# Layer 0's value product and its fillers in four TensorE tiles of 128 by 32 instead of two of 128 by 64

## The chip, the cores and the metric

The kernel runs on one NeuronCore of a Trainium2 chip. The metric is device time in microseconds. In three runs the kernel before took 2806.13 to 2808.9 us, with a median of 2807.47 us.

The engines are named as the profile names them: PE is TensorE's matmul, PEld its weight load, DVE is VectorE, ACT is ScalarE, POOL is GpSimd, and SP the queue that issues nearly all transfers. A name such as L514 is line 514 of the kernel.

TensorE's array has 128 rows (the contraction) and 128 columns (the partitions of the output). It can be used whole, or split into tiles: the profile's "128\*64" is a tile of 128 rows and 64 columns, two of which lie side by side, "128\*32" is one of four, "64\*64" one of four in a square, "32\*64" one of eight. Each instruction of the program addresses one tile, and tiles of one shape can run at once.

## What is computed

Two layers of cross-attention on a batch of four, all in float32. `x` is (4, 1024, 512), the context is (4, 1024, 384). Both layers have 16 heads; layer 0's are 64 wide, layer 1's 32 wide.

```python
def layer0(x, context):
    h = layernorm(x) * gamma + beta
    Q = (h @ Wq).reshape(B, NQ, 16, 64)
    K = (context @ Wk).reshape(B, NC, 16, 64)
    V = (context @ Wv).reshape(B, NC, 16, 64)
    attn = softmax(einsum('bihd,bjhd->bhij', Q, K)) * 64 ** -0.5
    vals = einsum('bhij,bjhd->bihd', attn, V).reshape(B, NQ, 1024)
    return x + vals @ Wo + bo

def layer1(x, context):
    xn = x * rsqrt(mean(x * x) + 1e-5) * norm_w
    q, k, v = xn @ wq, *split(context @ wkv)          # 16 heads of 32
    q, k = l2norm(rotate(q)), l2norm(rotate(k))
    attn = softmax(q @ k.T * sqrt(32))
    return x + (attn @ v) @ wout

out = layer1(layer0(x, context), context)
```

## The kernel before, in words

The four samples are worked through one after the other, each with layer 0 and then layer 1. In the profile a sample takes some 695 us: layer 0 about 450, layer 1 about 245.

**Layer 0** goes over 8 pairs of heads (a pair fills 128 partitions) and, within a pair, over 8 blocks of 128 queries. One step of `Attention0` (lines 462 to 491) makes the scores of one block for both heads (line 453, in 64\*64 tiles, 512 columns at a time), DVE takes each row's maximum (478), ACT the exponential (479), POOL divides by the sum (484), DVE turns 32 by 32 squares over (487), and 16 transfers regroup the squares of two blocks into the transposed probabilities `eT` (498). `product` (506 to 522) multiplies two blocks' `eT` with the values: for each of 8 blocks of 128 keys and each of the two heads, the head's 64 columns of `v` are the stationary operand, and 256 queries stream through (line 514). The two heads fill the two column halves of the array. The moving operand `eT[:, j, :, :, k * 32 : (k + 1) * 32]` is read in runs of 32 numbers. Products follow the scores by some blocks and are called in odd steps (490).

**Fillers.** After its scores, each step lets PE do other work while DVE and ACT work on the softmax. In the first layer's pairs that go by rows (`by_rows`, line 899), even steps do row-split products (`rows`, line 186, in 64\*64 tiles like the scores), and odd steps the values of a pair ahead. In the other pairs `work.fill` takes units from a queue, each with a price in microseconds written by hand (0.86 for a 512-column step, 0.66 for a block of values, 0.44 for half a step). The prices are constants and decide which units are taken in which step.

**The helper.** All these fillers but the row-split ones and the transposes go through `matmul` (167 to 172). It cuts the output's 128 columns into `which["cols"]` tiles and issues one product for each. `which["cols"]` is 2 while layer 0 is built and is set to 4 at line 1054 for layer 1, whose own product (line 741) has 32 columns for each of four heads, and back to 2 at line 1125. The helper serves the projections of queries and keys (`pqT`, `pkT`), the values (`pv`), the output product (`po`), and layer 1's projections (`k_p`, `q_p`); some of layer 1's first ones (`k_p`, and `pv` from `wkv`) are built while layer 0 still runs.

**Layer 1** goes over 4 groups of four heads, 256 queries and 256 keys at a time: scores in 32\*64 tiles (692), exponential on ACT (702), sums of probabilities on DVE (711 to 715), product with the values in 128\*32 tiles (741), with the second half of layer 1's projections, the output product and the next sample's first work as fillers (`self.u.fill`, 706).

All instructions of one engine run in the order of the program. One written float32 product becomes two weight loads and two MATMUL instructions in the profile.

Of the kernel before, what the change touches and what calls it, by code (L numbers as in the profile page):

```python
# [38 lines left out]
P = 128  # L39
# [7 lines left out]
HD0 = 64  # L47
# [61 lines left out]
def xattn_kernel(ctx: ExitStack, tc: tile.TileContext, a: dict, out: bass.AP):  # L109
# [13 lines left out]
        return ps_s.tile(list(shape), F32, tag="s", name=name)  # L123


    which = {"n": 0, "from": 0, "cols": 2, "reads": 0}
    read = [0, 0, 0, 0]
    held = {}

    def bank(name):  # L130

        which["n"] = min(range(which["from"], 4), key=lambda n: read[n])
        res = ps_f.tile([P, 512], F32, tag=f"f{which['n']}", name=name)
        held[id(res)] = res, which["n"]
        read[which["n"]] = float("inf")
        return res

    def free(pp, late=0.5):

        which["reads"] += 1  # L140
        read[held.pop(id(pp))[1]] = work.clock + late + 1e-6 * which["reads"]

    def evac(dst, src):
        nc.scalar.copy(dst, src)
# [8 lines left out]
    cols = const.tile([P, 3, NQ], F32, name="cols")  # L153
# [282 lines left out]
    BQ = 2  # L436
    r = [slice(j * HD0, (j + 1) * HD0) for j in range(2)]

    class Attention0:
# [66 lines left out]
        def product(self):  # L506
            p, q, pr, eT = self.blocks.popleft()
            W = BQ * P
            if q == 0:
                pr["vals"] = sb.tile([P, S], F32, tag="vals", bufs=4, name=f"vals0_{self.b}_{p}")  # L510
            av = bank(f"av_{self.b}_{p}_{q}")
            for k in range(NT):
                for j in range(2):
                    nc.tensor.matmul(  # L514
                        av[r[j], :W].rearrange("p (t a i) -> p t a i", t=BQ, a=4),
                        pr["v"][:, k, r[j]],
                        eT[:, j, :, :, k * 32 : (k + 1) * 32],
                        start=k == 0,
                        stop=k == NT - 1,
                    )  # L520
            evac(pr["vals"][:, q * W : (q + 1) * W], av[:, :W])
            free(av)
# [371 lines left out]
    for b in range(B):  # L894
# [14 lines left out]
        for p in range(NPAIR):  # L909
            later = 17.3 * (p == 0)  # L910
            other = []
            if p in by_rows:
                if p < 2:
                    outs = tail
                elif p % 2 == 0:
                    i = p // 2 - 1
# [3 lines left out]
                        lambda n, i=i: wo[i][:, n % 2, :],  # L920
# [45 lines left out]
            elif p % 2 == 0:  # L966
                i = p // 2 - 1
# [3 lines left out]
                    lambda n, i=i: wo[i][:, n % 2, :],  # L971
# [3 lines left out]
            if p == 6:  # L975
                kq, v = {}, []
# [7 lines left out]
                k = rotated_chains(lambda kq=kq: kq["k"], ct, NC_, lambda k, wk=wk: wk[:, k, :], f"k1_{b}_0", RowScratch())  # L984
# [15 lines left out]
            n = 7 * (p == 0)  # L1000
# [6 lines left out]
            for i in range(NT):  # L1007
# [10 lines left out]
                n = NT * (2 - p if p < 2 else NPAIR - p) - i  # L1018
# [32 lines left out]
        work.add(flat(outs[4:7]) + q[0][2] + outs[7])  # L1051
        work.drain()

        which["from"], which["cols"] = 1, 4
        att1 = Attention1(b, work)
        o = [
            sb.tile([P, S], F32, tag="vals", bufs=4, name=f"o1_{b}_{g}") if g < 2 else None
# [8 lines left out]
        for half in range(2):  # L1066
            n = 0
# [49 lines left out]
            kT, qT, v = kT1, qT1, att1.v1  # L1117
# [4 lines left out]
        att1.ended = True  # L1122
        att1.add_up()
        att1.quotient()
        which["from"], which["cols"] = 0, 2
        if b == B - 1:
            tail = flat(adds[1][4:])
        else:
# [42 lines left out]
```

## Time and profile before

| | |
|---|---|
| median of three runs | 2807.47 us |
| the profiled execution | 2810.92 us, of which the span from first to last instruction is 2808.9 us |
| granted TensorE clock | 0.999 of full speed |
| line 514 (product with the values) | 4096 MATMULs of 128\*64, mean 382 ns |
| its weight loads | 4096 of 64 columns, mean 137 ns |
| line 453 (layer 0's scores) | 4096 MATMULs of 64\*64, mean 598 ns |
| line 172 (the helper) in 128\*64 | 5008 MATMULs, of 128, 256 and 512 columns |
| line 172 in 128\*32 (layer 1) | 4800 MATMULs, of 128, 256 and 512 columns |
| line 741 (layer 1's product) | 4096 MATMULs of 128\*32, mean 386 ns |
| its weight loads | 4096 of 32 columns, mean 109 ns |
| transfers | 349.90 MB, mean 125 GB/s |

The instructions overlap: a MATMUL lasts 380 ns from its start to its modelled end, while the next on the same tile starts earlier. The mean of one is thus not what one costs, and the busy time of a group is the union of its instructions.

### The profile page before, as it was taken

To read this page: it belongs to the slowest core of one execution; us is meant where nothing else is said; L and a number is where in the kernel's file an instruction comes from. 1 tells how busy PE (TensorE), PEld (TensorE's weight loads), DVE (VectorE), ACT (ScalarE), POOL (GpSimd) and SP (SyncE) were. 2 spreads that over 40 slices of the span, in tenths; PEclk is the share of its full clock that TensorE was granted. 3 is DMA by queue.
4 is the path that set the end of the run, shared out by engine and by line. 5 is a ranking of instruction groups with operands and counts; after the bars stand their busy time and mean duration, and the time that the engine had idled before them with its cause. 6 is when DMAs were issued, how large, how long until landed. Compare 5 with 4: busy or idle time off the path is not lost.

```text
span 2808.9 us, 82714 instructions
## 1 busy us (share of the span) xinstructions
PE 2781.3 (99%) x35344; PEld 1391.0 (50%) x35344; DVE 2242.8 (80%) x3010; ACT 1436.3 (51%) x2323; POOL 945.1 (34%) x776
## 2 busy tenths in 40 slices
PE   9999999999999999999999999999999999999999
PEld 4444445555444444554454444455445444445543
DVE  5677786899777778699877777869987777886988
ACT  4444443766544444476644444446664444445665
POOL 2343354430234335342023433444202343353410
PEclk9999999999999999999999999999999999999999
DMA  5788777010388877501048888750105887874000
GB/s 141 175 196 188 183 168 162 23 38 27 73 204 193 191 186 167 143 23 38 27 95 203 196 188 190 157 128 23 38 27 119 200 196 180 188 162 110 3 3 32
DMA packets 177615, 349.90 MB, mean 125 GB/s; under 512 B 37600, under 2 KB 93152, under 8 KB 177248
## 3 DMA queue, kind: packets, MB, share of 16 engines
q1 hardware_dynamic: 176848, 344.42, 51.9%
q8 instruction: 278, 4.55, 0.7%
q14 instruction: 89, 0.73, 0.1%
q10 hardware_dynamic: 400, 0.20, 0.0%
HBM read 67.64 MB, written 8.39 MB: 27 GB/s over the span
## 4 chain that ended last, share of the span: by engine, by line
PE 74%; DVE 7%; ACT 2%; issue 1%; DMA 1%; POOL 0%; SPq 0%; DVEq 0%; ACTq 0%
PE s L453 13%; PE av L514 12%; PE s L692 8%; PE pv L172 7%; PE av L741 6%; PE po L172 6%; PE po L194 4%; PE pqT L194 4%; PE pkT L194 3%; PE k_p L172 3%; PE q_p L172 2%; DVE both L711 2%; ACT e L702 1%; PE pqT L172 1%; PE pkT L172 1%
## 5 line engine op out<-in xcount | busy, mean ns | idle before, releaser
L478 DVE TENSOR_REDUCE m<-s 128x1 f32<-128x1024 f32 x512 | 602.8, 1219 | 359.3 <-PE s L453 356.2
L702 ACT ACTIVATE e<-s 128x1024 f32<-128x1024 f32 x512 | 496.7, 1022 | 289.1 <-PE s L692 246.1
L479 ACT ACTIVATE e<-s,m 128x1024 f32<-128x1024 f32 x256 | 282.8, 1109 | 465.5 <-DVE m L478 281.3
L453 PE MATMUL s<-qk 64*64 64x512 f32 x4096 | 516.8, 598 | 3.2 <-ACT raw L479 0.9
L484 POOL TENSOR_SCALAR raw<-raw,li 128x1024 f32<-128x1024 f32 x256 | 286.1, 1118 | 693.5 <-DVE li L483 685.0
L479 ACT ACTIVATE raw<-s,m 128x1024 f32<-128x1024 f32 x256 | 285.1, 1114 | 369.2 <-DVE m L478 366.0
L514 PE MATMUL av<-eT,v 128*64 128x256 f32 x4096 | 470.1, 382 | 1.8 <-DMA eT<-e 1.7
L484 POOL TENSOR_SCALAR e<-e,li 128x1024 f32<-128x1024 f32 x256 | 286.3, 1120 | 472.1 <-DVE li L483 269.4
L514 PEld LDWEIGHTS av<-eT,v 128*64 128x64 f32 x4096 | 285.0, 137 | 228.2 <-issue 64.2
L711 DVE TENSOR_TENSOR both<-e 128x512 f32<-128x512 f32 x512 | 338.0, 692 | 55.6 <-ACT e L702 53.6
L487 DVE STREAM_TRANSPOSE e<-e 128x1024 f32<-128x1024 f32 x256 | 309.9, 1228 | 0.2
L487 DVE STREAM_TRANSPOSE e<-raw 128x1024 f32<-128x1024 f32 x256 | 309.9, 1228 | 0.0
L692 PE MATMUL s<-q,k 32*64 32x256 f32 x8192 | 302.6, 388 | 7.2 <-ACT e L702 5.9
L453 PEld LDWEIGHTS s<-qk 64*64 64x64 f32 x4096 | 150.8, 132 | 255.9 <-issue 197.7
L692 PEld LDWEIGHTS s<-q,k 32*64 32x64 f32 x8192 | 157.3, 131 | 163.7 <-ACT e L702 80.2
L172 PE MATMUL pv<-wv,cT 128*64 128x128 f32 (+1 forms) x3360 | 189.6, 273 | 1.5 <-ACT k L590 1.4
L172 PEld LDWEIGHTS pv<-wv,cT 128*64 128x64 f32 (+1 forms) x3360 | 174.0, 132 | 31.3 <-issue 15.0
L713 DVE TENSOR_TENSOR both<-both 128x1024 f32<-128x1024 f32 x128 | 162.6, 1271 | 4.4
L194 PE MATMUL pqT<-hT,w 64*64 64x512 f32 x1408 | 159.5, 589 | 0.0
L741 PE MATMUL av<-e,rest 128*32 128x256 f32 x2048 | 137.8, 387 | 0.0
L741 PE MATMUL av<-e,v 128*32 128x256 f32 x2048 | 137.0, 385 | 0.0
L172 PE MATMUL q_p<-wq,hT 128*32 128x256 f32 (+1 forms) x1920 | 126.1, 379 | 0.0
(99 smaller groups left out, 3071.8 us busy)
## 6 DMA issues: line engine op xcount, KB each, us to landing
eT<-e SPq DMA_DIRECT2D x2048, 128.0 KB, 2.4
xr<-in_x_dram SPq DMA_DIRECT2D x32, 256.0 KB, 4.1
w<-in_Wq_dram SPq DMA_DIRECT2D x32, 256.0 KB, 3.3
x<-in_x_dram SPq DMA_DIRECT2D x32, 256.0 KB, 3.0
wo<-in_Wo_dram SPq DMA_DIRECT2D x16, 512.0 KB, 4.3
out_dram<-x SPq DMA_DIRECT2D x32, 256.0 KB, 2.5
c<-in_ctx_dram SPq DMA_DIRECT2D x32, 192.0 KB, 3.7
wv<-in_Wv_dram SPq DMA_DIRECT2D x32, 192.0 KB, 3.4
```

Source lines behind the costliest of these rows:

```text
L172: nc.tensor.matmul(o[rr], lhsT[:, rr], rhs, start=start, stop=stop)
L194: nc.tensor.matmul(o["pp"][cc], o["lhsT"](k)[rr, cc], o["rhs"](k)[rr], start=first and k == 0, stop=not first and k == n - 1,)
L453: nc.tensor.matmul(sc[j][part : part + HD0, kb * 512 : (kb + 1) * 512], pr["qT"][r[j], i * P + part : i * P + part + HD0], pr["kT"][r[j], ...
L478: nc.vector.tensor_reduce(m[:, j : j + 1], sc[j], AX.X, ALU.max, negate=True)
L479: nc.scalar.activation(e[j], sc[j].rearrange("p (g s) -> p g s", g=4), AF.Exp, bias=m[:, j : j + 1], accum_out=l[:, j : j + 1])
L484: nc.gpsimd.tensor_scalar(e[j], e[j], li[:, j : j + 1], HD0**-0.5, ALU.mult, ALU.mult)
L487: self.turn = [lambda j=j: nc.vector.transpose(self.e[:, :, i % BQ * 2 + j, :], e[j]) for j in range(2)]
L514: nc.tensor.matmul(av[r[j], :W].rearrange("p (t a i) -> p t a i", t=BQ, a=4), pr["v"][:, k, r[j]], eT[:, j, :, :, k * 32 : (k + 1) * 32], ...
L692: nc.tensor.matmul(sc[j // 2][part : part + HD0, j % 2, c, :], kT[rr, g, k * P + part : k * P + part + HD0], qT[rr, g, qb * WQ : (qb + 1) ...
L702: nc.scalar.activation(e, sc[u], AF.Exp, scale=float(np.sqrt(np.float32(HD1))))
L711: nc.vector.tensor_add(into[:, 2 * u : 2 * u + 2, :], es[u][:, :, 0, :], es[u][:, :, 1, :])
L741: nc.tensor.matmul(self.av[rr, 0, :], v[g][:, 2 * kk + c, rr], es[j // 2][:, j % 2, c, :], start=first and c == 0, stop=end and c == 1,)
```

## The change

The column width of the helper `matmul` is 4 throughout, where it was 2 in layer 0 and 4 in layer 1. The product of layer 0 is written with four 32-column pieces for each block of keys instead of two 64-column ones; the pieces 0 and 1 take the first head's probabilities, 2 and 3 the second's.

```diff
-    which = {"n": 0, "from": 0, "cols": 2, "reads": 0}
+    which = {"n": 0, "from": 0, "cols": 4, "reads": 0}
...
             for k in range(NT):
-                for j in range(2):
+                for f in range(0, P, 32):
                     nc.tensor.matmul(
-                        av[r[j], :W].rearrange("p (t a i) -> p t a i", t=BQ, a=4),
-                        pr["v"][:, k, r[j]],
-                        eT[:, j, :, :, k * 32 : (k + 1) * 32],
+                        av[f : f + 32, :W].rearrange("p (t a i) -> p t a i", t=BQ, a=4),
+                        pr["v"][:, k, f : f + 32],
+                        eT[:, f // HD0, :, :, k * 32 : (k + 1) * 32],
                         start=k == 0,
                         stop=k == NT - 1,
                     )
...
-        which["from"], which["cols"] = 1, 4
+        which["from"] = 1
...
-        which["from"], which["cols"] = 0, 2
+        which["from"] = 0
```

## The prediction

> **What bounds the kernel now.** I read the page's first and fourth parts, to see which engine sets the end.
>
> ```profile
> span 2808.9 us, 82714 instructions
> PE 2781.3 (99%) x35344; PEld 1391.0 (50%) x35344; DVE 2242.8 (80%) x3010; ACT 1436.3 (51%) x2323; POOL 945.1 (34%) x776
> ...
> PE 74%; DVE 7%; ACT 2%; issue 1%; DMA 1%; POOL 0%; SPq 0%; DVEq 0%; ACTq 0%
> PE s L453 13%; PE av L514 12%; PE s L692 8%; PE pv L172 7%; PE av L741 6%; PE po L172 6%; PE po L194 4%; PE pqT L194 4%; PE pkT L194 3%; PE k_p L172 3%; PE q_p L172 2%; DVE both L711 2%; ACT e L702 1%; PE pqT L172 1%; PE pkT L172 1%
> ```
>
> TensorE (PE) is busy almost without a gap, and the chain of waits runs through it. A busy PE may be one that runs slowly, so I then asked for the busy time by stage: one sample's layer 0 (735 to 1175 us) and the layer 1 behind it.
>
> ```profile
> core 0: us, PE busy (x) PEld busy (x) DVE busy (x) ACT busy (x) POOL busy (x), PEclk, DMA share, GB/s
> 735.00:1175.00 440.00, 439.53 (x4212) 220.22 (x4214) 341.96 (x457) 193.80 (x366) 179.89 (x158) 1.00 0.78 182
> 1182.00:1426.00 244.00, 241.97 (x4611) 122.71 (x4600) 213.87 (x288) 162.75 (x210) 52.45 (x33) 1.00 0.10 29
> ```
>
> In layer 0, where nearly all of the change lies, PE is busy for 439.53 of 440 us at full clock, and the next engine (DVE) for 342. So what a visit of PE to the changed column tiles costs is what counts. That needs both kinds of tile, which the groups by shape set side by side (busy us, then mean ns of one):
>
> ```profile
> L514 PE MATMUL av<-eT,v 128*64 128x256 f32 x4096 | 470.1, 382 | 1.8 <-DMA eT<-e 1.7
> L172 PE MATMUL pv<-wv,cT 128*64 128x128 f32 x2784 | 171.2, 273 | 1.4 <-ACT k L590 1.4
> L741 PE MATMUL av<-e,v 128*32 128x256 f32 x2048 | 137.0, 385 | 0.0
> L172 PE MATMUL pv<-wv,cT 128*32 128x128 f32 x576 | 18.4, 273 | 0.1
> ```
>
> One written product stands as two MATMULs: line 514 makes 4 x 8 x 4 x 8 x 2 = 2048 and shows 4096. The busy times here are unions of overlapping instructions, and short bursts inflate them, so they can't be divided by counts; starts can. From the single starts in the trace, the same column tile takes its next instruction every 216 ns at 256 columns, 109 ns at 128 and 429 ns at 512, **in 128*64 and in 128*32 alike** (call that a slot). Timeline rows, start and length, show the same with the ends of each visit:
>
> ```profile
> 383.45 1.95 PE L453 MATMUL s<-qk 64*64 64x512 f32 x16
> 385.32 3.67 PE L514 MATMUL av<-eT,v 128*64 128x256 f32 x32
> 388.83 0.83 PE L172 MATMUL pv<-wv,cT 128*64 128x128 f32 x12
> 389.58 1.95 PE L453 MATMUL s<-qk 64*64 64x512 f32 x16
> ...
> 517.02 1.07 PE L741 MATMUL av<-e,v 128*32 128x256 f32 x16
> 518.02 1.09 PE L283 MATMUL pth<-ident,xn 128*128 128x128 f32 x8
> ...
> 653.25 1.49 PE L172 MATMUL pv<-wv,cT 128*32 128x128 f32 x48
> 654.68 1.12 PE L692 MATMUL s<-q,k 32*64 32x256 f32 x32
> ```
>
> A 128*64 visit: 385.32 to 389.58 is 4.26 us, and 16 slots of 0.216 and 6 of 0.109 make 4.11, so 0.15 is left over. A 128*32 visit: 517.02 to 518.02 is 1.00, four slots make 0.86, and 0.14 is left over. The 48 values in 128*32 take 1.43 for 12 slots (1.31) and the way out. Nothing grows with length; only the ends of a visit differ.
>
> **The change part by part.** *What it converts.* L514's 4096 MATMULs, and all 128*64 rows of the helper at L172: 2784 + 512 + 576 + 768 + 128 + 96 + 128 + 16 = 5008 (pv of both layers' weights, po of vals, k_p, pqT, pkT, q_p, po of o). That makes 9104 more MATMULs and as many weight loads, 18,208 instructions. "All fillers" is not literally so: the row-split products of L194 (64*64) and the transposes (128*128) are not built by this helper and stay. No DMA, no evacuation and no wait is added or moved, and the planner's prices are constants, so the order of work stays.
>
> *Inside a visit: 0.* Half the columns per tile, twice the tiles, the same slot: 216, 109 and 429 ns in both.
>
> *Entering.* The first weight load of a new shape can't hide, and the first MATMULs are longer by it:
>
> ```profile
> L514 PE MATMUL av<-eT,v x4096: 378/379/431, 62.6 to 2562.6; 128*64 128x256 f32 x196
> L741 PE MATMUL av<-e,v x2048: 379/379/404, 491.1 to 2690.5; 128*32 128x256 f32 x187
> ```
>
> 431 - 379 = 52 against 404 - 379 = 25 ns; in starts, the first slot is 51 longer in 128*64 and 24 in 128*32. Entering gains 27 ns.
>
> *Leaving.* From the last MATMUL's start, the next shape starts one slot plus 88 to 95 ns later, whichever two shapes meet (93 from L514 to 64*64, 93 from L741 to 128*128, 93 in the three passages from 128*32 to 64*64). But the tiles of one slot start 6.7 ns apart, so the last of four starts 20 ns after the first, and of two 6.7: leaving loses 13.5 ns. Net per visit 27 - 13.5 = 13.5 ns gained, as 151 against 137 ns left over.
>
> The Trainium skill, "TensorE: Matmul & The Clock Gate", section "Measured speedup vs the span model", puts the spacing of tiles at about 4 ns; by it, as an estimate, leaving would lose 8 and the net be 19 ns, but the starts above measure 6.7. The same page speaks against the change in "Wait — 56ns, not 53.3ns?": with hardware decode off the sequencer spends about 62 ns per MATMUL. An estimate by it: four MATMULs would take 248 ns, 32 more in each of 2400 slots of 256 columns and 139 more in each of 1776 of 128, some 324 us slower; the values in 128*32 refute it here with 109 ns per four.
>
> *How many visits.* Merging PE's MATMULs in order of time by tile shape gives 203 visits in 128*64: 170 entered from 64*64, 32 from a transpose, one from 128*32. 203 x 13.5 = 2.74 us. Where PE waits for something else before its next such visit, the gain is swallowed: 43 of them have a wait over 30 ns there, and 160 x 13.5 = 2.16. I take **2.5 us**. The wait that swallows is line 453's for its score bank (ACT behind DVE); that is what is late next.
>
> *Not shown before, with bounds.* (a) The entry from 64*64 into 128*32 does not occur before. All entries into 128*32 are 22 to 25 and all exits of 64*64 86 to 88, so +-7 ns on 170 visits, +-1.2 us; I take 0. (b) Line 514 reads its moving operand in runs of 32 numbers, and four tiles will read it where two did. Nearest rows: L514 with two tiles 216, L741 with four tiles on unbroken rows 216. Between nothing and a slot doubled (2048 x 0.216 = 442 us); I take nothing, as both nearest rows give 216. (c) Instruction supply: the slower rival below, 0 to 24 us; I take 0. (d) Downwards: if entering cost nothing at all, 203 x 51 ns = 10.4 us less.
>
> Sum, against the profiled execution: span 2808.9, with 2.0 around it 2810.92, becomes 2806.4 and 2808.4. That execution stands 3.45 us above the median 2807.47 of the runs (2806.13 to 2808.9), so I take the difference from the median: **2805.0 us**, 0.09% down.
>
> **The rivals.** *Slower: instruction supply.* The page has
>
> ```profile
> q8 instruction: 278, 4.55, 0.7%
> ```
>
> 278 packets of 16 KB for 70,688 PE instructions are one per 256, and 18,208 more need 71 more. Beside it stand DMA engines 78% busy in layer 0 against 10% in layer 1. In one place of one sample's layer 1 (1352 us) the values in 128*32 stop for 450 instead of 109 ns, with no releaser, right after a fetch that started late; the other samples don't stop there. If every added fetch cost these 0.34 us, 71 x 0.34 = 24 us: **2829**. It makes the kernel slower by 0.2% from 24 of the 71 on (8.1 us over 0.34). Against it: layer 0 now has 8426 PE instructions in 440 us and would have some 12,980, 256 in 8.7 us; layer 1 draws 9211 in 244 us, 256 in 6.8 us, and runs through. A fetch takes 0.9 to 1.8 us in the trace even under layer 0's traffic.
>
> *Slower: the strided operand* of (b): from 4 ns per slot (8.2 us over 2048) it would decide; at 10 ns **2825**.
>
> *No gain at all.* PE's head start is lost each time at line 453's score bank: **2807.5**. For it: those 43 visits. Against it: all of PE's waits in layer 0, by the starts, come to some 33 of 1800 us.
>
> *More gain*: with nothing of the entry left, **2797**. Against it: the 24 ns that L741 still pays.
>
> **How the numbers follow.** The forecast has 0.72, no gain 0.08, supply 0.10, the strided operand 0.04, more gain 0.06. A measurement of this kernel can tell about 0.2%, 5.6 us, from no change. The forecast's own range is 2802 to 2808 (2.2 to 2.7 gained, +-1.2 of (a), and the spread of the runs). The whole range, 2800 to 2811, takes in a third of the larger gain below and some ten late fetches above. Faster by over 0.2%: 0.07; within: 0.79 (forecast and no gain, less a point of tail); slower: 0.14.
>
> **What would show it.** L514 as 128*32 x8192 with a longest first MATMUL near 404 in place of 431; weight loads near 110 ns, not 137; slots still 216 and 109; visits with 0.137 left over; PE x44448; some 349 fetches in the page's third part. Supply would show as stops inside visits with no releaser, the strided operand as L514 slots over 216 with L172's at 216. I am wrong if the slot itself moves, for then thousands of slots count where I counted 203 ends.

## The result

The changed kernel takes 2818.49 us (median of five runs, 2814.63 to 2819.58), against 2807.36 us (2806.13 to 2808.9) before. The ratio is 1.0035 with a 95% interval of 1.0022 to 1.0049: 11 us slower, where 2.5 us faster was forecast, and above the range.

The page of the changed kernel, its first, third and fourth parts (shares of the span by engine, the queue of PE's instruction fetches, the chain of waits):

```profile
span 2816.5 us, 100922 instructions
PE 2776.8 (99%) x44448; PEld 1352.9 (48%) x44448; DVE 2243.4 (80%) x3010; ACT 1436.2 (51%) x2323; POOL 944.8 (34%) x776
...
q8 instruction: 349, 5.72, 0.9%
...
PE 67%; DVE 8%; SPq 4%; DMA 3%; ACT 2%; issue 2%; POOL 0%; DVEq 0%; ACTq 0%
PE s L453 11%; PE av L514 11%; PE s L692 8%; PE av L741 6%; PE pv L172 6%; PE po L172 6%; SPq L498 4%; PE pqT L194 3%; PE po L194 3%; PE pkT L194 2%; PE q_p L172 2%; DMA eT<-e 2%; PE k_p L172 2%; DVE both L711 2%; ACT e L702 1%
```

PE has the 44448 MATMULs and the queue the 349 fetches that were forecast, and PE's busy time fell by 4.5 us (2781.3 before) while the span grew by 7.6. The chain shows what is new: SP's issue of the regrouping transfers (SPq L498) and their flight (DMA eT<-e), 6% of the span between them, neither of which stood among the chain's lines before. Two groups of the changed kernel (busy us, mean ns of one, idle before):

```profile
L514 PE MATMUL av<-eT,v 128*32 128x256 f32 x8192 | 468.6, 380 | 14.3 <-DMA eT<-e 9.4
L172 PE MATMUL pv<-wv,cT 128*32 128x128 f32 x6144 | 190.4, 273 | 1.4 <-ACT k L590 1.4
```

The product's busy time fell by 1.5 us, but PE stood idle before it for 14.3 us in place of 1.8, most of it until a transfer into `eT` landed. The view of line 514 (duration min/median/max) has the shorter entry that was forecast:

```profile
L514 PE MATMUL av<-eT,v x8192: 376/379/404, 61.4 to 2570.2; 128*32 128x256 f32 x200
```

404 where it was 431. So PE does what was reckoned, and something before it got later. The view of line 498, the regrouping's issues and waits on SP, first before the change, then after it:

```profile
L498 SPq DMA_DIRECT2D eT<-e x2048: 507/590/2217, 45.4 to 2551.7; - x187
L498 SPq EVENT_SEMAPHORE  x128: 17/1304/21187, 16.1 to 2542.2; - x128
...
  POOL e L484: 189.5, 47
  ACT e L479: 121.3, 31
  PE av L514: 1.7, 2
...
DMA to landing us min/median/max: 2.2/2.4/7.0
```

```profile
L498 SPq DMA_DIRECT2D eT<-e x2048: 507/590/2290, 44.2 to 2562.7; - x187
L498 SPq EVENT_SEMAPHORE  x128: 17/966/21174, 15.8 to 2552.1; - x128
...
  POOL e L484: 231.0, 58
  ACT e L479: 137.0, 36
  PE av L514: 9.4, 10
...
DMA to landing us min/median/max: 2.2/2.9/7.3
```

SP issues 16 transfers of 0.59 us for every two blocks and then waits for the next ones to be written. The median of that wait fell from 1304 to 966 ns. A transfer takes 2.9 us to land in the median, not 2.4. POOL, ACT and PE stand with longer waits for it (us, times). For POOL and ACT this only changes which wait ended last: all waits before these two groups come to 463.4 and 465.5 us before the change and to 461.4 and 463.8 after it. What grew is PE's. SP's issuing is no busy time in the profile's first part, so the engine table of the prediction did not have this queue in it. From the single starts in the two traces, within the 22 pairs by rows:

| | before | after |
|---|---|---|
| time of a pair | 52.6 us | 52.8 us |
| SP issuing, per pair | 42.0 us | 43.5 us |
| PE fetches, per pair | 4.14 | 5.86 |
| issues of eT longer than 0.8 us, whole kernel | 119 | 171 |
| from eT's last landing to its product, median | 1.81 us | 1.32 us |
| products that start late, of 128, and their delay in all | 5, 2.1 us | 22, 15.8 us |

A product counts as late where it starts over 15 ns behind the 90 ns that PE takes from the scores to the next shape where nothing interferes. Each late one starts within 0.5 us of the last landing in its `eT`, so that this is what it waited for. 1.5 us more of issue for 1.72 more fetches is 0.87 us for each. Of the 171 long issues, 165 have a fetch of PE's instructions that began during them or up to 1.5 us before; of the 1877 short ones 140. Before the change it is 112 of 119 and 81 of 1929.

PE's own account, made by taking the slots, entries and exits of the prediction off the starts of all visits: entries cost 36.9 us instead of 42.3 and exits 113.7 instead of 111.1, together 2.8 us less, and what remains, the waits, 77.1 instead of 67.5, 9.6 more. That is the result's sign and nearly its size: 6.8 of the 7.6 us of these two executions. The late products alone make 13.7 us more; PE's other waits fell by some 4. Line 453 does not wait longer than before: the idle time before it was 3.2 us and is 3.0.

### The profile page after: what moved, and what is told of

Read it like the earlier page. It is cut to its first block, busy times and chain, and to the rows that moved or that the text cites. A ratio compares the mean times of both kernels' runs of the same rounds, so it can differ in the third digit from the quotient of the medians.

```text
span 2816.5 us, 100922 instructions
## 1 busy us (share of the span) xinstructions
PE 2776.8 (99%) x44448; PEld 1352.9 (48%) x44448; DVE 2243.4 (80%) x3010; ACT 1436.2 (51%) x2323; POOL 944.8 (34%) x776
## 4 chain that ended last, share of the span: by engine, by line
PE 67%; DVE 8%; SPq 4%; DMA 3%; ACT 2%; issue 2%; POOL 0%; DVEq 0%; ACTq 0%
PE s L453 11%; PE av L514 11%; PE s L692 8%; PE av L741 6%; PE pv L172 6%; PE po L172 6%; SPq L498 4%; PE pqT L194 3%; PE po L194 3%; PE pkT L194 2%; PE q_p L172 2%; DMA eT<-e 2%; PE k_p L172 2%; DVE both L711 2%; ACT e L702 1%
## 5 line engine op out<-in xcount | busy, mean ns | idle before, releaser
L479 ACT ACTIVATE e<-s,m 128x1024 f32<-128x1024 f32 x256 | 283.0, 1110 | 463.8 <-DVE m L478 259.4
L514 PE MATMUL av<-eT,v 128*32 128x256 f32 x8192 | 468.6, 380 | 14.3 <-DMA eT<-e 9.4
L514 PEld LDWEIGHTS av<-eT,v 128*32 128x32 f32 x8192 | 262.8, 110 | 259.4 <-issue 72.5
L172 PE MATMUL pv<-wv,cT 128*32 128x128 f32 x6144 | 190.4, 273 | 1.4 <-ACT k L590 1.4
L172 PEld LDWEIGHTS pv<-wv,cT 128*32 128x32 f32 x6144 | 171.3, 110 | 32.9 <-issue 14.7
L172 PE MATMUL q_p<-wq,hT 128*32 128x256 f32 x2048 | 126.1, 379 | 0.0
```

The lines of the kernel that those rows point to most:

```text
L172: nc.tensor.matmul(o[rr], lhsT[:, rr], rhs, start=start, stop=stop)
L479: nc.scalar.activation(e[j], sc[j].rearrange("p (g s) -> p g s", g=4), AF.Exp, bias=m[:, j : j + 1], accum_out=l[:, j : j + 1])
L514: nc.tensor.matmul(av[f : f + 32, :W].rearrange("p (t a i) -> p t a i", t=BQ, a=4), pr["v"][:, k, f : f + 32], eT[:, f // HD0, :, :, k * 3 ...
```

## The experiments

**Theory A**: the 71 added fetches hold up SP's issues, `eT` lands later, and PE, ACT and POOL wait for it. **Theory B**: four tiles that read the moving operand slow the transfers. The prediction's own rival was a third: PE starves of instructions.

### More instructions without another tile: split256 and after_split256

```diff
-            for kb in range(2):
+            for kb in range(4):
...
-                            sc[j][part : part + HD0, kb * 512 : (kb + 1) * 512],
+                            sc[j][part : part + HD0, kb * 256 : (kb + 1) * 256],
...
+                for h in range(2):
+                    hh = slice(h * 256, (h + 1) * 256)
...
-                        o["rhs"](k)[rr],
-                        start=first and k == 0,
+                            o["rhs"](k)[rr, hh],
+                            start=first and k == 0 and h == 0,
```

> The kernel before, its two-tile columns kept, but the scores (L453) and the row-split fillers (L194) are written in halves of 256 columns: 15,936 more PE instructions, some 62 more fetches of 256 instructions, no tile shape changed. PE's own price: a slot of 512 columns takes 429.3 ns and two of 256 take 431.5, on some 2000 slots, +4.3 us. Theory A (each fetch holds up SP's issue of the regrouping transfers, eT lands later, L514 waits): +4.3 and about 62 x 0.18 us (12.6 us over the 71 fetches of the change), 2823 us (2816 to 2832), with issues of eT longer than 0.8 us up from 119 to some 165. Theory B (four tiles reading the moving operand slow the transfers): only PE's price, 2812, long issues as before.

> The changed kernel with the same halves of 256 columns: another 62 fetches on top of the 71. Theory A: SP has no room left in layer 0's pairs by rows, so each fetch costs between 0.18 and 0.8 us: 2818.5 + 4.3 + 11 to 50, 2834 to 2870. Theory B: 2823, PE's price alone.

split256 took 2828.94 us, a ratio of 1.0069 (1.0057 to 1.0082), within theory A's range; but its time alone does not tell the theories apart. Its starts show a price on PE that was not reckoned: some 84 places in the row products with 60 ns more and some 72 passages from the scores with 50 ns more. With the slots that is about 13 us, the greater part of the loss. The rest goes the way of theory A: 14 products start late, by 7.9 us in all, where it was 5 and 2.1, and the long issues rise to 145, for 340 fetches, though no tile is changed. after_split256 took 2847.53 us, 1.0130 (1.0114 to 1.0145), within theory A's range too. That is 18.6 us over split256, where the change alone costs 11: the same 71 fetches seem to cost more where `eT` already lands later. 41 products start late, by 28.1 us in all, and from eT's landing to the product it is 0.69 us in the median.

### Where the loss is: outside4 and inside4

```diff
-            later = 17.3 * (p == 0)
-            other = []
+            later, other, which["cols"] = 17.3 * (p == 0), [], 2 if p in by_rows else 4
...
-                for j in range(2):
+                for f in range(0, P, P // which["cols"]):
+                    ff = slice(f, f + P // which["cols"])
```

inside4 has 4 and 2 in place of 2 and 4. Behind the pairs of layer 0, outside4 goes on with 4, and inside4 with 2 until layer 1 begins.

> Four tiles only outside layer 0's pairs by rows (the other pairs, layer 1's first work and the tail), two within them: some 8,400 of the 18,208 added instructions (33 fetches) and some 115 of the 203 visits. Theory A (fetches hold up SP, where SP has no room): SP waits 5 to 20 us per pair there, so the fetches cost nothing and PE's 115 x 13.5 ns = 1.5 us show: 2804 to 2810. Theory B (four tiles slow the transfers everywhere): half of the loss, 2812 to 2815.

> Four tiles only within layer 0's pairs by rows, two elsewhere: some 9,900 added instructions (38 fetches), some 88 visits (-1.2 us). Theory A: the whole loss, as SP waits only 3 to 4 us of a pair's 53 here: 2816 to 2823. Theory B: the other half, 2812 to 2815.

outside4: 1.0001 (0.9992 to 1.0010), no difference, as theory A has it and theory B hasn't. inside4: 1.0015 (1.0006 to 1.0023), 4 us slower: the sign and the place are theory A's, the size is half of its lower bound. The two don't add up to the change's 11 us.

### SP relieved: before8 and after8

```diff
-            for g in range(4):
-                for k in range(4):
-                    nc.sync.dma_start(eT[32 * g : 32 * (g + 1), k], self.e[32 * k : 32 * (k + 1), g])
+            for g in range(2):
+                for k in range(4):
+                    nc.sync.dma_start(eT[64 * g : 64 * (g + 1), k], self.e[64 * (k % 2) : 64 * (k % 2 + 1), 2 * g + k // 2])
```

The regrouping goes in 8 transfers of 64 partitions instead of 16 of 32. The squares land in other places of `eT`, so these kernels compute other numbers; bytes and work are the same.

> The kernel before with the regrouping in 8 transfers of 64 partitions per two blocks instead of 16 of 32: the same bytes from the same tile into the same tile, but to other places, so the products read other numbers. If an issue costs SP per transfer, SP is busy for some 5 us of 12 instead of 10; PE sets the pace before: theory A 2800 to 2809.

> The changed kernel with the same 8 transfers per two blocks (same bytes, other places). Theory A: with SP's issue halved the fetches no longer count and PE's gain shows: 1 to 4 us below before8. Theory B: still 8 to 14 us above before8. If an issue costs by bytes (1.18 us each), SP isn't relieved and both theories say 8 to 14 above.

before8 took 0.9994 of before (0.9986 to 1.0003), after8 0.9996 (0.9987 to 1.0005). The page of after8:

```profile
span 2805.2 us, 99898 instructions
...
q8 instruction: 349, 5.72, 0.9%
...
eT<-e SPq DMA_DIRECT2D x1024, 256.0 KB, 5.9
```

All 349 fetches and all four-tile products are there, the same bytes move, and the loss is gone. SP issues for 28.9 us per pair by rows instead of 43.5, and none of the 128 products starts late. So neither the tiles nor PE's supply of instructions cost time as such; the loss goes through the regrouping. Fewer transfers change more than SP's issue, though; the last experiment takes that apart. PE's gain doesn't show in the time: the medians are 2806.34 and 2806.14, and 2.5 us is within these intervals.

### SP relieved in a whole kernel: after_relieved, before_relieved, after_pool

```diff
+    queue = {"e": nc.sync}
...
+            queue["e"] = nc.scalar if p in by_rows else nc.sync
             if p in by_rows:
```

Weights, `x` and the stores then go through `queue["e"]`; after_pool has `nc.gpsimd` in place of `nc.scalar`.

> The changed kernel, but in layer 0's pairs by rows the transfers other than the regrouping (weights, x, stores, some 2.8 us of issue per pair of 53) are issued by ACT's queue instead of SP's. Theory A: SP gets back more room than the added fetches take (some 2 per pair at 0.8 us), eT is in time again, and PE's 2.5 us show: 2804 to 2809. Theory B, and the theory that PE starves of instructions: nothing of it changes, 2816 to 2820.

> The kernel before with the same transfers moved to ACT's queue: what the move does by itself. Theory A: SP had room, PE sets the pace, 2804 to 2809, at most a us or two less than before. Theory B: the same.

> The changed kernel with the transfers other than the regrouping in the pairs by rows issued by POOL's queue instead of SP's (ACT's queue lost 120 us, since ACT's exponentials stood behind the issues). Theory A: SP has 2.8 us more per pair and eT is in time, 2804 to 2809, unless POOL's scaling (L484) is held up behind the issues as ACT's exponentials were: then slower than 2818.

All three missed: 1.051 (1.0492 to 1.0528), 1.0439 (1.0424 to 1.0454) and 1.0138 (1.0123 to 1.0153). With ACT's queue the transfers stand in front of the exponentials, and the waits of ACT show it (us, times, longest), in after_relieved and in the changed kernel:

```profile
ACT e L480 <- DMA eT<-e: 242.7, 52, 7.0
```

```profile
ACT e L479 <- DMA eT<-e: 137.0, 36, 4.9
```

With POOL's queue SP issues less (40.7 us per pair by rows), and yet the transfers into `eT` land later; after_pool's list of issues:

```profile
eT<-e SPq DMA_DIRECT2D x2048, 128.0 KB, 4.0
```

4.0 us against 2.9. Why was not pursued; POOL's scaling isn't held up behind the issues, it starts 0.15 us after its factors are ready in the mean, against 0.14 in the changed kernel. As the moved transfers bring new waits, these runs don't decide on the fetches. But after_pool shows one thing: SP issues for less time than before the change (42.0 us), and yet 49 products start late. How long SP issues in all is not what decides. No version that beats the kernel before came out of the study.

### The place of a fetch: before_shift, after_shift, inside4_shift

```diff
     nc.gpsimd.memset(ones, 1.0)
+    lead = [score(f"lead_{i}") for i in range(2)]
+    for i in range(32): nc.tensor.matmul(lead[i % 2][:HD1, :8], ident[:, :HD1], ident[:, :8], start=True, stop=True)
```

> The kernel before with 32 small products at its start (32 columns by 8, results unread, 128 PE instructions), in the time in which PE waits for the first load: every later instruction moves by half a fetch, nothing else changes. If the place of a fetch within the regrouping matters, the time moves; before has room in SP, so by little: 2805 to 2811. If only the number of fetches counts: the same within 2 us.

> The changed kernel with the same 32 small products. Theory A says a loss of 8 to 14 us against before; if the place of the fetches matters too, it moves within 3 to 20 us (2810 to 2828); if only the number counts, it stays at 2815 to 2820.

> Four tiles in the pairs by rows alone, with the same 32 small products. Without them it lost 4 us where the changed kernel, whose instructions in these pairs are the same, lost 6 there. If the place matters: moves by 2 us or more from 2811.4, to the loss of the changed kernel or to none. If not: 2809 to 2814.

before_shift 0.9998 (0.9988 to 1.0007), after_shift 1.0026 (1.0016 to 1.0037), inside4_shift 1.0029 (1.0017 to 1.0041). The changed kernel's loss stands with every fetch moved by half of its length, at 6.6 us by the medians, under the 8 to 14 that were expected. inside4's went from 4 to 6 us, as much as after_shift's. The intervals overlap in both cases, so that the place of the fetches matters is possible and not shown.

### Fetches alone: before_nops, before_nops_half and their controls

```diff
                             start=True,
                             stop=True,
                         )
+                        for _ in range(2): nc.tensor.nop(hint="x", nofuse=True)
             return sc
...
                         stop=k == NT - 1,
                     )
+                    for _ in range(2): nc.tensor.nop(hint="x", nofuse=True)
             evac(pr["vals"][:, q * W : (q + 1) * W], av[:, :W])
```

before_nops has 4 in place of 2.

> The kernel before with its two-tile columns and 16,384 empty instructions (NoOp) on PE's sequencer, 4 after each score product and 4 after each value product: 64 more fetches (18,208 instructions and 71 fetches in the change), no tile, no wait and no work changed. Theory A (the number of fetches): a loss like the change's without its gain of 2.5, 8 to 16 us. Theory B (four tiles reading the moving operand): 2805 to 2811, none. If the empty instructions hold up PE itself, PE would stand still inside visits, and before8_nops would lose as much.

> The same empty instructions in before8 (regrouping in 8 transfers of 64 partitions, to other places). Theory A: SP has room for the fetches, so it stays at before8's 2803 to 2809. If the empty instructions hold up PE, it loses as before_nops does.

> Half of the empty instructions, 8,192, 32 fetches, two after each product. Theory A: between none and half of before_nops' loss, as half of SP's room is still there: 1 to 7 us. Theory B: none.

> The control for before_nops_half: the same 8,192 empty instructions, in before8 (regrouping in 8 transfers of 64 partitions, same bytes, other places). Theory A: the 32 fetches meet room in SP and the empty instructions cost PE nothing: 2803 to 2809, as before8. If the 6 us of before_nops_half are the empty instructions' own price on PE: 2811 to 2814.

With four empty instructions after each product PE itself is slowed: before_nops takes 1.0633 (1.0618 to 1.0647) and the control before8_nops 1.0644 (1.0629 to 1.0658), so these two say nothing of the fetches. With two, PE's slots stay at 216, 109 and 429 ns. The page of before_nops_half and its views of lines 515 (514 before) and 522, the empty instructions:

```profile
span 2813.9 us, 90906 instructions
...
q8 instruction: 310, 5.08, 0.8%
...
eT<-e SPq DMA_DIRECT2D x2048, 128.0 KB, 2.6
```

```profile
L515 PE MATMUL av<-eT,v x4096: 379/379/431, 62.2 to 2567.6; 128*64 128x256 f32 x196
```

```profile
L522 PEldq NOP  x4096: 13/13/13, 61.1 to 2565.7; - x196
```

32 fetches more, two tiles, no work changed, and it takes 1.0024 (1.0014 to 1.0034), 6 us more. Long issues rise from 119 to 153, and from eT's landing to the product it is 1.48 us in the median, not 1.81. 15 products start late, by 5.8 us in all. In the control before8_nops_half, with 8 transfers, one does, and the time is 1.0001 (0.9992 to 1.0010). **That shows the cause**: fetches of PE's instructions, with no tile changed, cost time with the 16 transfers, and nothing with 8.

Where on the way the fetches act can be read off the traces: from the last squares written by DVE (line 487) to the last landing in `eT`, in means over the 88 regroupings of the pairs by rows (us):

| | squares to landing | first issue to end of last | from there to landing | late products, whole kernel |
|---|---|---|---|---|
| before | 13.11 | 10.95 | 2.06 | 5, 2.1 us |
| after | 13.80 | 11.38 | 2.27 | 22, 15.8 us |
| before_nops_half | 13.53 | 11.31 | 2.06 | 15, 5.8 us |
| before8 | 12.73 | 6.51 | 6.16 | 2, 0.3 us |
| after8 | 13.03 | 6.61 | 6.35 | none |
| before8_nops_half | 12.87 | 6.61 | 6.20 | 1, 0.2 us |

The added fetches lengthen the way by 0.69 us in the change and by 0.42 in before_nops_half, of which 0.43 and 0.36 lie in SP's issue and 0.21 and nothing in the flight behind it; the small rest is the start of the first issue. With 8 transfers they lengthen it too, by 0.30 and 0.14, but it begins 0.4 us shorter, and after8 ends where before does. So 8 transfers do two things: they make the fetches cost less, and they let `eT` land earlier. SP isn't full in any of the six: in the median it begins a regrouping 0.06 us after the squares are written, and it waits for 4.5 us per pair by rows before the change and 3.0 after it. Its issues stand in series between the squares and the product, and that series got longer.

## Why the prediction was wrong

- **The bound.** "PE is busy for 439.53 of 440 us" was right, and PE did set the pace before. But "the next engine (DVE) for 342" left out the path that stood closest behind: from the squares through SP's 16 issues to `eT`, 13.1 us for each regrouping, which ended 1.81 us before the product in the median and in 5 cases too late. The engine table doesn't count issuing, and no view of SP was read.
- **Inside a visit, entering, leaving.** Right: slots of 216, 109 and 429 ns, entries of 24 ns in place of 51, exits as before. 2.8 us came out in PE's account for 2.74 reckoned.
- **The step that failed** is "(c) Instruction supply: the slower rival below, 0 to 24 us; I take 0", with "No DMA, no evacuation and no wait is added or moved" before it. 71 fetches are transfers. The rival had the right cause in its hand, 71 more fetches against a busy DMA system, but sought its price at PE, as stops within visits with no releaser. The change added none: stops of over 70 ns between the slots of a visit come to 34.1 us before and 33.8 after, and after8 has the same fetches and no loss. The price is paid on the way of `eT`, for the most part in SP's issue, some 0.87 us per fetch there, and reaches PE as the wait of L514: 22 late products and 15.8 us in place of 5 and 2.1.
- **Its chance and its size.** It got 0.10 and 2829; the loss was 11 us for 71 fetches, 14 with PE's gain taken off, or 0.2 us each; before_nops_half has 6 for 32, the same. The range ended 7.5 us short of the result. That PE's waits in layer 0 "come to some 33 of 1800 us" was used to show that a gain passes through; it doesn't say how close the next path stands. That is the time from eT's landing to its product, which was not looked at.
- **The strided operand** cost nothing: L514's slots are 216 ns.
- **The page's rules.** The 62 ns per MATMUL that the Trainium skill ("TensorE: Matmul & The Clock Gate", section "Wait — 56ns, not 53.3ns?") gives for hardware decode off are again not what the trace shows: 109 ns per four in the median of the 6144 MATMULs of the values. Whether decode was on, no run here shows.

Open: what in a fetch lengthens SP's issue, and in the change the flight after it (that they coincide is shown, the resource between them isn't), and why outside4 and inside4 together lose 4 us and the change 11. The traces say where the difference lies: of the changed kernel's late products 7 with 4.2 us lie outside the pairs by rows; outside4 has 3 with 1.3 us there, and inside4 none.

## What to carry to other kernels

An instruction count is a load on the transfers: where a change doubles instructions at equal work, count the fetches that it adds and look for transfers that land just before their use. A table of busy engines leaves out a queue that only issues, and a queue that is not full can still be a link in series; for SP, add up the way from the data to the last landing, issues and flight, and see how long before its use each transfer lands. A gain of 13 ns per visit isn't worth 18,000 instructions there.

## What the runs showed of the hardware that was not expected

- PE fetches 256 instructions at a time (349 fetches of 16 KB for 88,896), each taking 1.0 us in the median, and an issue on SP beside it often takes 0.8 to 2.3 us in place of 0.59.
- Two empty instructions after each product hide behind PE (before8_nops_half, 1.0001), four do not: 6% of the time (before8_nops, 1.0644), though the trace shows 13 ns for each.
- The 32-column tiles of float32 products have no throughput of their own to offer: 216 ns per 256 columns and 109 per 128 with two tiles and with four.
- A transfer of 64 partitions and 256 KB costs SP's queue 0.77 us in the mean, one of 32 partitions and 128 KB 0.64 (before8 and before): per byte, fewer and larger transfers relieve it. They take longer to land, 5.7 us in the median against 2.4, so that the way from the squares to the last landing is only 0.4 us shorter (12.73 against 13.11).
